# Cross attention on one core: another order of the first four blocks, with the division moved behind the values, seven-product projections from block 0, earlier loads and moves issued from two queues

## The chip, the core and the metric

The kernel runs on one core of a Trainium2 chip. The metric is device time in microseconds, the median of several runs. A core has five engines that work side by side and meet only through semaphores: TensorE (PE in the profile; its weight loads are listed apart as PEld), VectorE (DVE), ScalarE (ACT), GpSimd (POOL) and SyncE (SP, which here only issues transfers). Each engine executes its own queue strictly in the order in which the program was written, so an instruction that waits holds up all that stands behind it on the same engine. Transfers run on 16 DMA engines. PE writes to PSUM, eight banks of 128 partitions by 512 f32 numbers; the other data lie in SBUF.

## What is computed

Sixteen sequences x of 1024 rows by 512 features attend to 64 context rows each. Everything is f32. Cut to what matters:

```python
def _ada_ln(x, c, W_ss, b_ss):
    h = (x - mean(x)) / sqrt(var(x) + 1e-5)
    scale, bias = split(silu(c) @ W_ss + b_ss, 2)
    return (1.0 + scale)[:, None, :] * h + bias[:, None, :]

xq  = _ada_ln(x_q,  t_vec, Wss_q,  bss_q)
xkv = _ada_ln(x_kv, t_vec, Wss_kv, bss_kv)
q = (xq @ Wq + bq).reshape(B, Lq, 16, 32)
k, v = halves of (xkv @ Wkv + bkv), 16 heads of 32
scores = einsum('bqhd,bkhd->bhqk', q, k) / sqrt(32)
attn = softmax(scores)
out = einsum('bhqk,bkhd->bqhd', attn, v).reshape(B, Lq, 512)
return x_q + (out @ Wp + bp)
```

## The kernel before

**Tiling.** A block is 512 rows of x, so there are 32 blocks, two to a sequence. Keys and values are made for two sequences (four blocks) at a time. The work is software-pipelined: while block i is in its scores, block i-1 is multiplied with the values, block i-2 is projected, and blocks i+1 to i+5 are loaded, normalised, transposed and turned into queries. The schedule is written out by hand. It has three parts: the **way in** (lines 955 to 1136: the preparation and the scores of blocks 0 to 3), a loop `for i in range(4, NB - 2)` from line 1139 on, and a way out. The change edits the way in and a few helpers that it calls; loop and way out stay as they are.

**The steps of a block**, with the names that the schedule uses:

- `load_x(i)` loads 1 MB (tag `x`, two buffers); `load_residual(i)` loads the same rows again for the residual sum (tag `r`, two buffers). All loads are issued by SP.
- `q_stats(i)` computes mean and variance on DVE. `q_scale(i)` makes the reciprocal deviation: two or five small ACT steps, then four small steps on POOL (argument `apart` true) or on DVE. `hidden(i, ts)` normalises on ACT, in place, a quarter block at a time.
- `turn(i, ts)` transposes 32x32 squares on DVE into a tile `ht`; `move(i)` (line 502) then carries the squares to their partitions with 16 DMAs of 64 KB into `xt`, which holds features by rows.
- `queries(i, o)` (line 533) multiplies one quarter of the query features on PE and has ACT write it to `qt` (`queried`). The later form needs seven quarter-size products for the whole block instead of eight: `query_product(i, n)`, with sums of halves that `query_weight_sums` and `feature_sums` make on POOL, a seed copied by ACT (`query_seed`) and results read out by ACT (`query_out`) and DVE (`query_added`).
- `scores(i, z)` does half of the keys: PE writes two PSUM tiles of two banks (tag `s`, which has only two such tiles), DVE takes the maxima, ACT copies the scores to SBUF. `crossed=True` has ACT begin with the second tile while DVE begins with the first; on the same tile the two follow one another. `maxima(i)` joins the maxima and spreads them over a tile; `subtract(i)` subtracts them, on POOL or DVE, two operations of 128x2048; `weights(i, z)` is the exponential on ACT.
- The division of the softmax comes in two forms. **Before the values:** `sums` (DVE), `inverse` (DVE: reciprocal and a spread of 128x2048) and `divide` (POOL, two operations of 128x2048), then `mix(i)` multiplies with the values on PE and `mixed(i)` copies the result with ACT. **Behind the values:** `mix` takes undivided weights; meanwhile `total` (POOL) and `row_total` (DVE) sum them, `inverse_rows` takes reciprocals and brings them to their partitions through DRAM (one DMA out, four in), `spread_rows` spreads them on DVE and `divided(i)` multiplies on DVE while reading PSUM.
- The projection comes in two forms too. `project(i, t)` takes four steps of a quarter of the rows, each joined to the residual by DVE (`projected`), with the bias added to the residual rows by POOL (`residual`). The other form has **seven products**: `product(i, n)`, n = 1 to 7, in two accumulators, banks 2 and 3. `biased(i, k)` has ACT seed an accumulator with the bias (k = 2) or the difference of two bias halves (k = 3), `row_sums` makes sums of halves on POOL, and `added(i, n)` has DVE add the state of the accumulator to its part of the output after each product. So product n+1 in the same bank waits for `added(i, n)`. `weight_sums` prepares the weight sums once, on POOL.
- Banks 0 to 3 are dealt out by `ring`; once the seven-product projection runs, the ring is cut to banks 0 and 1.

**Where each form was used before the change.** Blocks 0 to 2 were divided before the values, blocks from 3 on behind them. Blocks 0 and 1 used `project`, blocks from 2 on the seven products. Blocks 0 to 4 used `queries`, blocks from 5 on the seven products. `load_x(3)`, `load_residual(0)` and the projection's weights and bias were loaded between `hidden(1)` and `queries(0, 2)`.

Of the kernel before, what the change touches and what calls it, by code (L numbers as in the profile page):

```python
# [9 lines left out]
F32 = mybir.dt.float32  # L10
# [5 lines left out]
P = 128  # L16
# [4 lines left out]
def cross_attention_block(  # L21
# [16 lines left out]
):  # L38

# [99 lines left out]
    def load_x(i):  # L139
        t = xpool.tile([P, NT, H], F32, tag="x", name=f"x_{i}")  # L140
        nc.sync.dma_start(t, rows_of(x, i))
        x_tiles[i] = t
# [34 lines left out]
    for c in range(NC):  # L177
        nc.sync.dma_start(
            b_v_sb[c * 32 : (c + 1) * 32, :],
            b_kv[H + c * P : H + (c + 1) * P].rearrange("(o h) -> o h", o=1).to_broadcast([32, P]),  # L180
        )
# [123 lines left out]
    def q_scale(i, kvb=None):  # L305
        n = NT if kvb is None else NT + 1
        q_rstd[i] = rstd_of(q_mv.pop(i)[:, :n, :], n, "q", i > 1)
        if kvb is not None:
            kv_rstd[kvb] = (q_rstd[i], NT)
# [180 lines left out]
    def turn(i, ts):  # L490

        if ts[0] == 0:
            ht_tiles[i] = hpool.tile([P, 4, NC, NT, 32], F32, tag="ht", name=f"ht_{i}")
# [8 lines left out]
    def move(i):  # L502
# [3 lines left out]
        for k in range(4):  # L506
            for g in range(4):
                nc.sync.dma_start(  # L508
# [24 lines left out]
    def queries(i, o, later=False):  # L533
        xt, b = xt_tiles[i], i // BPB
        w = wq_tiles.get(b, w_q_sb)
        if o == 0:

            tag = "vb" if i in (1, 3) else "qt"
            qt_tiles[i] = qpool.tile([P, NC, TB], F32, tag=tag, name=f"qt_{i}", bufs=1)
# [13 lines left out]
    def queried(i, o):  # L553
        pq, b = pq_tiles.pop((i, o)), i // BPB
        dst = qt_tiles[i][:, o, :]
# [194 lines left out]
    def inverse(i):  # L750
# [4 lines left out]
        vb_tiles[i] = spread(i, v, f"vb_{i}", other=i in (1, NB - 1))  # L755
# [15 lines left out]
    def row_total(i):  # L771
# [7 lines left out]
        )  # L779

# [187 lines left out]
    query_bias_rows()  # L968
    kv_stats(0)
# [10 lines left out]
    load_x(2)  # L980
    load_residual(0)
    load_projection_bias()
# [5 lines left out]
    load_x(3)  # L988
# [7 lines left out]
    keys(0)  # L996
    hidden(2, range(NT))


    scores(0, 0)  # L1000
    turn(2, range(NT))
    move(2)
    load_context(2)
    load_x(4)
    load_residual(1)
    residual(0)
    value_products(0)
    scores(0, 1)
    maxima(0)
    subtract(0, nc.vector, (0,))  # L1010
    value_tiles(0)
    subtract(0, nc.vector, (1,))
    queries(1, 0)
    query_weights(1)
    queries(1, 1)
    weights(0, 0)
    queries(1, 2)
    weights(0, 1)
    sums(0, 0)
    queries(1, 3)  # L1020
    query_weight_sums()
    sums(0, 1)
    inverse(0)
    divide(0)
    scores(1, 0)
    queries(2, 0)
    q_stats(3)
    queries(2, 1)
    q_scale(3)
    scores(1, 1)  # L1030
    maxima(1)
    subtract(1)
    queries(2, 2)
    hidden(3, (0, 1))
    mix(0, apart=False)
    mixed(0)
    hidden(3, (2, 3))
    queries(2, 3)
    turn(3, range(NT))
    move(3)  # L1040
    kv_stats(2)
    q_stats(4)
    project(0, 0)
    weights(1, 0)
    sums(1, 0)
    project(0, 1)
    weights(1, 1)
    residual(1)


    load_x(5)
    q_scale(4)
    kv_scale(2)
    scores(2, 0)
    sums(1, 1)
    inverse(1)
    divide(1)
    project(0, 2)
    context_hidden(2)
    hidden(4, (0, 1))  # L1060
    scores(2, 1)
    maxima(2)
    subtract(2)
    weight_sums()
    hidden(4, (2, 3))
    project(0, 3)
    queries(3, 0)
    queries(3, 1)
    queries(3, 2)
    turn(4, range(NT))  # L1070
    load_residual(2)
    move(4)
    mix(1)
    mixed(1)
    q_stats(5)
    weights(2, 0)
    queries(3, 3)
    project(1, 0)
    sums(2, 0)
    weights(2, 1)  # L1080
    project(1, 1)
    sums(2, 1)
    inverse(2)
    divide(2)
# [3 lines left out]
    project(1, 2)  # L1088


    load_x(6)
    scores(3, 0, crossed=True)
    project(1, 3)
    ring[:] = [0, 1]
    scores(3, 1)
    maxima(3)
    subtract(3)
    queries(4, 0)
    load_residual(3)
    hidden(5, (0, 1))  # L1100
    biased(2, 2)
    mix(2)
    mixed(2)
    hidden(5, (2, 3))
    q_stats(6)
    turn(5, range(NT))
    move(5)
    q_scale(6)
    row_sums(2, 0)
    load_x(7)  # L1110
    queries(4, 1)
# [3 lines left out]
    weights(3, 0)  # L1115
    added(2, 2)
    biased(2, 3)
    weights(3, 1)
    total(3)
    queries(4, 2)  # L1120
    keys(2)
    hidden(6, range(NT))
    scale_features(5)
    row_sums(2, 1)
# [209 lines left out]
```

## Time and profile before

| what | value |
|---|---|
| median of 3 runs | 1059.04 us (1056.97 to 1059.98) |
| the profiled execution | 1058.86 us |
| its span, first to last instruction | 1057.1 us |
| mean granted TensorE clock | 0.998 |
| DVE busy, 50 to 60 us and 100 to 110 us | 9.83 and 9.76 of 10 us |
| POOL busy, 10 to 30 us | 0 of 20 us |
| DMA share, 10 to 30 us | 1.04 |
| the loop's first scores, scores(4,0), start on PE | 161.96 us |

The page lists busy time per engine, the busy tenths of 40 slices of the span, the DMA queues, the chain of work that ended last (followed back from the last instruction, each step to what released it), and the costliest groups of instructions. A timeline shows instructions in the order of their start: start, length in us, engine, line, operation, output and inputs with their shapes, how many were merged (x), and in brackets how long the engine had been idle and what ended that. "PE busy" covers matmuls whose ends are modelled, so a busy PE can still wait a little inside a merged row. Times in tables and text count from the start of the span.

The chain of waits shows how closely the engines hang together at the beginning of the kernel (start us, us, what):

```
64.53 1.41 DVE vb L716
65.94 1.02 issue
66.96 0.02 POOLq L760
66.98 9.01 POOL s L760 x2
75.99 0.17 POOL workq L282
```

### The profile page before, as it was taken

The numbers are of one execution on the slowest core, as the hardware profiler recorded it, in microseconds if no ns is written. First come the engines' busy times: TensorE is split into PE (matmuls) and PEld (weight loads), VectorE is DVE, ScalarE is ACT, GpSimd is POOL, SyncE is SP. The second block draws the span as 40 slices with busy tenths as digits, with TensorE's granted clock in tenths as the row PEclk, the third lists the DMA queues.
The fourth block names the chain that finished last, engine by engine and source line by source line (L and its number), as shares of the span: only waits on it lengthen the run. The fifth ranks groups of instructions, "written<-read, shape, count | busy, mean of one in ns | idle before, by whom it ended". The sixth has DMA issues, their size and how long they took to land.

```text
span 1057.1 us, 22537 instructions
## 1 busy us (share of the span) xinstructions
PE 1033.6 (98%) x8914; PEld 733.7 (69%) x8914; DVE 854.7 (81%) x1134; ACT 618.0 (58%) x951; POOL 752.7 (71%) x470
## 2 busy tenths in 40 slices
PE   6999998999999999999999999999999999999998
PEld 4534365777777787777787787777777777777433
DVE  5698648987789877888878878898778887776993
ACT  3566665665575655667556666566566765565330
POOL 0258794889768869788668986688886886787340
PEclk9999999999999999999999999999999999999999
DMA  9743444444535344544345443444454443334202
GB/s 337 248 127 111 130 122 127 155 150 147 161 94 162 123 140 145 171 148 127 106 131 164 153 158 112 126 141 150 139 157 134 152 134 116 98 115 162 82 30 90
DMA packets 99976, 147.27 MB, mean 139 GB/s; under 512 B 29944, under 2 KB 30096, under 8 KB 99872
## 3 DMA queue, kind: packets, MB, share of 16 engines
q1 hardware_dynamic: 99872, 145.85, 43.5%
q8 instruction: 70, 1.15, 0.5%
q14 instruction: 34, 0.28, 0.1%
HBM read 78.85 MB, written 34.44 MB: 107 GB/s over the span
## 4 chain that ended last, share of the span: by engine, by line
PE 80%; DVE 5%; POOL 5%; DMA 4%; SPq 2%; issue 2%; ACT 1%; POOLq 0%; DVEq 0%; ACTq 0%
PE pp L933 28%; PE pq L625 27%; PE po L825 6%; PE ps L673 6%; PE pp L852 5%; PE pq L542 3%; SPq L508 2%; PE pv L431 2%; PE pk L395 2%; POOL s L760 2%; DMA wss_kv<-in_L_xcond_Wss_kv_dram 2%; DMA b_p_sb<-in_L_xcond_bp_dram 1%; POOL s L729 1%; DMA x<-in_x_dram 1%; DVE s L729 1%
## 5 line engine op out<-in xcount | busy, mean ns | idle before, releaser
L729 POOL TENSOR_TENSOR s<-s,mb 128x2048 f32<-128x2048 f32 x58 | 263.1, 4560 | 160.8 <-DVE mb L716 160.8
L694 ACT COPY s<-ps 128x1024 f32<-128x1024 f32 x128 | 129.5, 1012 | 119.7 <-DVE m L685 82.9
L685 DVE TRANSPOSE_TENSOR_REDUCE m<-ps 128x32 f32<-128x1024 f32 x128 | 150.6, 1214 | 27.1 <-PE ps L673 27.1
L655 ACT ACTIVATE qt<-pq,bias_t 128x256 f32<-128x256 f32 x208 | 85.8, 463 | 110.9 <-PE pq L625 110.9
L933 PE MATMUL pp<-w_p_sb,ot 128*128 128x256 f32 x648 | 148.7, 379 | 0.0
L735 ACT ACTIVATE s<-s 128x2048 f32<-128x2048 f32 x64 | 122.3, 1911 | 42.4 <-POOL s L729 31.8
L947 DVE TENSOR_TENSOR r<-pp,r 128x512 f32<-128x512 f32 x189 | 122.5, 670 | 25.5 <-PE pp L933 19.8
L933 PEld LDWEIGHTS pp<-w_p_sb,ot 128*128 128x128 f32 x648 | 123.4, 190 | 17.4 <-issue 0.7
L768 POOL TENSOR_TENSOR sum<-s,s 128x2048 f32<-128x2048 f32 x27 | 122.7, 4543 | 0.8 <-ACT s L735 0.8
L933 PEld LDWEIGHTS pp<-WT,s 128*128 128x128 f32 x432 | 78.9, 192 | 54.0 <-issue 29.3
L933 PE MATMUL pp<-WT,s 128*128 128x256 f32 x432 | 109.3, 397 | 0.0
L933 PE MATMUL pp<-WT,ot 128*128 128x256 f32 x432 | 102.2, 380 | 0.0
L625 PE MATMUL pq<-xt_sums,wq_sums 128*128 128x256 f32 x416 | 101.0, 386 | 0.0
L321 ACT ACTIVATE x<-x,rstdq 128x512 f32<-128x512 f32 x128 | 96.7, 807 | 4.8 <-POOL rstdq L285 3.2
L625 PE MATMUL pq<-xt,wq_sums 128*128 128x256 f32 x416 | 99.0, 381 | 0.0
L625 PEld LDWEIGHTS pq<-xt_sums,wq_sums 128*128 128x128 f32 x416 | 77.0, 190 | 31.1 <-issue 21.8
L625 PE MATMUL pq<-xt,w_q_sb 128*128 128x256 f32 x416 | 98.4, 380 | 0.1
L260 DVE BATCH_NORM_STATS2 bs<-x 128x6 f32<-128x512 f32 x128 | 86.9, 679 | 5.0 <-DMA x<-in_x_dram 5.0
L662 DVE TENSOR_TENSOR qt<-pq,qt 128x256 f32<-128x256 f32 x104 | 39.1, 418 | 63.1 <-PE pq L625 62.5
L933 PEld LDWEIGHTS pp<-WT,ot 128*128 128x128 f32 x432 | 82.2, 190 | 11.0
L565 ACT ACTIVATE xt<-xt,ss_q 128x512 f32<-128x512 f32 x112 | 84.7, 810 | 6.1 <-DMA xt<-ht 4.3
L625 PEld LDWEIGHTS pq<-xt,w_q_sb 128*128 128x128 f32 x416 | 79.1, 190 | 11.0 <-PE pp L933 0.4
(139 smaller groups left out, 1725.0 us busy)
## 6 DMA issues: line engine op xcount, KB each, us to landing
x<-in_x_dram SPq DMA_DIRECT2D x32, 1024.0 KB, 6.4
r<-in_x_dram SPq DMA_DIRECT2D x32, 1024.0 KB, 5.5
xt<-ht SPq DMA_DIRECT2D x496, 64.0 KB, 2.0
out_dram<-r SPq DMA_DIRECT2D x54, 512.0 KB, 3.8
out_dram<-r SPq DMA_DIRECT2D x20, 256.0 KB, 2.0
wss_q<-in_L_xcond_Wss_q_dram SPq DMA_DIRECT2D x2, 1024.0 KB, 8.8
ctx<-in_ctx_dram SPq DMA_DIRECT2D x8, 256.0 KB, 3.2
wss_kv<-in_L_xcond_Wss_kv_dram SPq DMA_DIRECT2D x2, 1024.0 KB
```

The source lines that it names most:

```text
L260: nc.vector.bn_stats(bs, r)
L321: nc.scalar.activation(dst, src, AF.Identity, bias=rstd[:, 1, j : j + 1], scale=rstd[:, 0, j : j + 1])
L565: nc.scalar.activation(xt[:, :, c, :], xt[:, :, c, :], AF.Identity, scale=ss["q"][:, c, b : b + 1], bias=ss["q"][:, NC + c, b : b + 1],)
L625: nc.tensor.matmul(qa[k][:, m * HT : (m + 1) * HT].rearrange("p (g n) -> p g n", g=2), lhsT=a[:, c, m * P : (m + 1) * P], rhs=x[:, :, c, : ...
L655: nc.scalar.activation(dst, src, AF.Identity, bias=bq_t[:, o : o + 1])
L685: nc.vector.tensor_reduce(m_tiles[i][:, z, 2 * e : 2 * e + 2, :], pss[e].rearrange("p r (j a) -> p r j a", a=32), AX.X, ALU.max, apply_tra ...
L694: nc.scalar.copy(s_sb[:, 2 * e : 2 * e + 2, :], pss[e])
L729: eng.tensor_tensor(s_tiles[i, z], s_tiles[i, z], mb_tiles[i], ALU.subtract)
L735: nc.scalar.activation(p, p, AF.Exp, scale=SCALE)
L768: nc.gpsimd.tensor_tensor(t, s_tiles[i, 0], s_tiles[i, 1], ALU.add)
L933: nc.tensor.matmul(acc[k][:, t * HO : (t + 1) * HO], lhsT=rows[:, c, t * P : (t + 1) * P], rhs=cols[:, c, :], start=n == 2 and t == 0 and ...
L947: nc.vector.tensor_add(r, acc[k].rearrange("p (t h) -> p t h", t=2), r)
```

## The change

Helpers:

```diff
     def load_x(i):
-        t = xpool.tile([P, NT, H], F32, tag="x", name=f"x_{i}")
+        t = xpool.tile([P, NT, H], F32, tag="r" if i == 3 else "x", name=f"x_{i}")
...
-    for c in range(NC):
-        nc.sync.dma_start(b_v_sb[...], b_kv[...].to_broadcast([32, P]))
+    def load_value_bias():
+        for c in range(NC):
+            b = b_kv[H + c * P : H + (c + 1) * P].rearrange("(o h) -> o h", o=1)
+            nc.sync.dma_start(b_v_sb[c * 32 : (c + 1) * 32, :], b.to_broadcast([32, P]))
...
-        q_rstd[i] = rstd_of(q_mv.pop(i)[:, :n, :], n, "q", i > 1)
+        q_rstd[i] = rstd_of(q_mv.pop(i)[:, :n, :], n, "q", i > 3)
...
     def turn(i, ts):
-            ht_tiles[i] = hpool.tile([P, 4, NC, NT, 32], F32, tag="ht", name=f"ht_{i}")
+            pool, tag = (big, "big2") if i == 2 else (hpool, "ht")
+            ht_tiles[i] = pool.tile([P, 4, NC, NT, 32], F32, tag=tag, name=f"ht_{i}")
...
     def move(i):
-                nc.sync.dma_start(
+                (nc.gpsimd if i < 4 and k % 2 else nc.sync).dma_start(
...
+    def halves_total(i):
+        lt_tiles[i] = small.tile([P, HPC, NJ], F32, tag="lt", name=f"lt_{i}")
+        both(lt_tiles[i].rearrange("p r j -> p (r j)"), l_tiles.pop(i), ALU.add)
```

The tile `qt` is now allocated in `queried(i, 0)` and not in `queries(i, 0)`; only block 1 takes the buffer `vb` for it, and only block 31 the buffer `xt` for its spread.

So 8 of the 16 transfers of move(1), move(2) and move(3) are issued by GpSimd; x_3 goes to a buffer of the residual rows and is loaded early; x_2 is queued ahead of the value bias; and the steps of `q_scale` for blocks 2 and 3 run on DVE instead of POOL. Blocks 0 and 1 still sum their weights half by half on DVE (`sums`), then `halves_total` joins the halves for the division behind the values; block 2 uses `total` and `row_total`.

The new order from the keys of block 0 to the loop (all of `inverse`, `divide`, `mixed`, `project`, `residual` and the four `queries(4, ...)` are gone from it):

```python
    key_products(0, bank("pk_0")); hidden(2, range(NT)); q_stats(3)
    turn(2, (0,)); key_tiles(0); turn(2, (1, 2, 3)); move(2)
    load_x(4); load_residual(0); load_context(2)
    q_scale(3); hidden(3, range(NT)); value_products(0); value_tiles(0)

    scores(0, 0, crossed=True); queries(1, 0); turn(3, (0, 1)); scores(0, 1)
    maxima(0); turn(3, (2, 3)); subtract(0, nc.vector)
    queries(1, 1); query_weights(1); weight_sums(); queries(1, 2); weights(0, 0)
    queries(1, 3); move(3); load_x(5); load_residual(1)
    weights(0, 1); query_weight_sums(); ring[:] = [0, 1]
    sums(0, 0); scores(1, 0, crossed=True); sums(0, 1); halves_total(0); inverse_rows(0)
    queries(2, 0); scores(1, 1); maxima(1); subtract(1); queries(2, 1); queries(2, 2)
    biased(0, 2); mix(0); spread_rows(0); divided(0)
    weights(1, 0); queries(2, 3); weights(1, 1); row_sums(0, 0)
    q_stats(4, kvb=2); q_scale(4, kvb=2)
    product(0, 1); added(0, 1); product(0, 2); added(0, 2); row_sums(0, 1); sums(1, 0)

    scores(2, 0, crossed=True); biased(0, 3); hidden(4, (0, 1))
    queries(3, 0, later=True); sums(1, 1); halves_total(1); inverse_rows(1)
    scores(2, 1); queried(3, 0); hidden(4, (2, 3)); maxima(2); subtract(2)
    product(0, 7); queries(3, 1); turn(4, range(NT)); move(4); load_x(6)
    added(0, 7); product(0, 6); added(0, 6); product(0, 5); added(0, 5)
    product(0, 4); added(0, 4); product(0, 3); added(0, 3); load_residual(2)
    biased(1, 2); mix(1); spread_rows(1); divided(1)
    context_hidden(2); queries(3, 2); weights(2, 0); row_sums(1, 0); q_stats(5)
    queries(3, 3); weights(2, 1); total(2); q_scale(5)
    context_features(2); scale_features(4)
    product(1, 1); added(1, 1); product(1, 2); added(1, 2); row_sums(1, 1)
    biased(1, 3); feature_sums(4); row_total(2); inverse_rows(2)

    scores(3, 0, crossed=True); product(1, 7); query_product(4, 1); query_seed(4)
    added(1, 7); scores(3, 1); hidden(5, (0, 1, 2)); product(1, 6); added(1, 6)
    maxima(3); subtract(3); query_product(4, 2); query_out(4, 2)
    product(1, 5); added(1, 5); product(1, 4); product(1, 3); hidden(5, (3,))
    spread_rows(2); added(1, 4); added(1, 3); biased(2, 2); load_residual(3)
    mix(2); divided(2); row_sums(2, 0); turn(5, range(NT)); move(5); load_x(7)
    query_product(4, 6); weights(3, 0); query_out(4, 6); q_stats(6)
    product(2, 1); added(2, 1); product(2, 2); added(2, 2); q_scale(6)
    weights(3, 1); total(3); query_product(4, 7); query_out(4, 7)
    biased(2, 3); row_sums(2, 1); key_products(2, spare("pk_2")); hidden(6, range(NT))
    query_product(4, 5); query_added(4, 5); key_tiles(2); turn(6, range(NT)); load_x(8)
    query_product(4, 4); query_added(4, 4); scale_features(5)
    value_products(2, spare("pv_2")); q_stats(7); value_tiles(2)
    query_product(4, 3); query_out(4, 3); feature_sums(5)
    product(2, 7); row_total(3); inverse_rows(3); move(6); q_scale(7)
```

(Several calls are put on one line here; the program has one to a line.)

Ahead of that, `load_x(2)`, `load_value_bias()` and `load_x(3)` stand right behind `query_bias_rows()`, and the projection's weights and bias are loaded behind `move(1)`.

## The prediction

> **What bounds the kernel now.** I read the page's busy shares and slices first, then each engine's timeline over 0 to 190 us; the loop over blocks 4 to 13 is not edited. TensorE (PE) is busy in 98% of the span, so little can be won unless its work or its few gaps shrink. The page, then PE's timeline (start, length, instructions, in brackets the idle time before them and what ended it):
>
> ```profile
> PE 1033.6 (98%) x8914; PEld 733.7 (69%) x8914; DVE 854.7 (81%) x1134; ACT 618.0 (58%) x951; POOL 752.7 (71%) x470
> ```
>
> ```profile
> 46.53 14.26 PE L542 MATMUL pq<-xt,wq 128*128 128x512 f32 x32 [0.97 <-DMA xt<-ht]
> ...
> 109.27 2.35 PE L825 MATMUL po<-s,vt 32*32 32x512 f32 x64
> ...
> 165.94 1.97 PE L625 MATMUL pq<-xt,w_q_sb 128*128 128x256 f32 x8
> 170.84 1.25 PE L673 MATMUL ps<-qt,kt 32*32 32x512 f32 x32 [2.94 <-ACT s L694]
> 172.02 3.56 PE L933 MATMUL pp<-WT,s 128*128 128x256 f32 x8
> ```
>
> The way in is already close to PE-bound: from 18.1 us to scores(4,0) at 161.96 PE shows about 6 us of gaps and stretched waits. Then 2.94 us pass before scores(4,1), and the next product takes 3.56 us where two take 3.45 elsewhere. The windows (length, busy time per engine, granted clock, DMA share, GB/s) say why: the clock was halved.
>
> ```profile
> 172.00:174.00 2.00, 2.00 (x12) 1.62 (x6) 2.00 (x3) 0.68 (x1) 0.00 (x0) 0.50 0.31 63
> ```
>
> What opens that gap is a chain from VectorE (DVE) over SyncE (SP): turn(5), 16 issues of move(5), then x_7, whose statistics stand in DVE's queue ahead of the maxima of scores(4,0):
>
> ```profile
> 143.31 2.49 DVE L495 STREAM_TRANSPOSE ht<-x 128x512 f32<-128x512 f32 x4 [0.19 <-ACT x L321]
> ...
> 161.90 0.69 DVE L260 BATCH_NORM_STATS2 bs<-x 128x6 f32<-128x512 f32 x1 [0.89 <-DMA x<-in_x_dram]
> ```
>
> ```profile
> 145.86 10.02 SPq L508 DMA_DIRECT2D xt<-ht  x16
> 155.97 5.43 SPq L141 DMA_DIRECT2D x<-in_x_dram  x2
> ```
>
> From the end of turn(5) (145.80) to scores(4,1) (170.84) it is 25.0 us; the new code has these steps in the same order.
>
> **Prices**, start to start in these timelines: a query chunk 3.55 (14.19/4); a product 1.77 (the loop takes 29.2 us a block; less scores 2.16 and mix 2.28, over 14 products); a project 3.5; a scores half 1.08; mix 2.28. On DVE: sums 2.2, a pair of maxima 2.3, spread 2.3, turn 2.45, added 0.65, q_stats 3.2. On ScalarE (ACT): exponential 1.85, a copy of scores 1.0. On POOL: a 128x2048 operation 4.5, a 128x512 one 1.27.
>
> **What goes.** Three stages become seven products: projections 0 and 1, query 4. Each saves 4x3.5-7x1.77 = 1.6 (query: 1.8), together 5.1 us of PE, 3.3 of it before mix(2). POOL loses two divisions (9.0 us) for each of blocks 0 to 2 and two residual additions (5.0 each). Most of that lay beside PE work: mix(0), mix(1) and mix(2) show about 1.5, 0 and 0.45 us of waiting, so it is worth 2 us, not 27.
>
> **What comes.** DVE gets divided (2.36 a block) where ACT copied, three more added per projection, and query_added. Two row sums and total(2) go to POOL, the accumulator seeds (0.57) to ACT. Loads of x_2 and x_3 are queued earlier, but the DMA engines moved 380 to 400 GB/s from 10 to 34 us: x_2 came 13 us after its issue, behind bytes that stay. I take 0.4 us earlier (0 to 1), and x_3 where r_0 came, by 38.
>
> **Moves from two queues.** 24 DMAs are issued by POOL; the trace has none there. Lower bound nothing; the nearest row is SP's 0.63 each; upper bound 2 us. [...] Then move(3) starts once queries(1,3) frees its buffer (62.2), its 8 issues and query_weight_sums (5.1) end at 75.3, and subtract(1), queued behind them, has its maxima at 75.9: free up to 1.07 us an issue. At 0.63 nothing changes. At 2 us subtract(1) is 7.4 late, less some 2 of slack: +5. [...] In the row above 8 issues fewer are 5 us. By the row move(1) lands 5 us earlier, [...] it removes at most the 0.97 at 46.53, because queries(1,0) now comes first at 44.
>
> **The walk**, each engine's new order laid out with those prices.
>
> Up to mix(0). x_2 lands 33.5; statistics 3.25, rstd 1.55, q_stats(3) 3.25, turn and key_tiles 3.2, rstd(3) 0.75: hidden(3) starts on ACT at 45.6 and holds it 2.9 us, with the copies of scores(0,0) queued behind. Those free the PSUM of scores(0,1) at 50.6, while PE finished queries(1,0) at 47.6: gap A, 2.9. Behind it the exponential delays queried(1,3): 1.2. Mix(0) ends at 78.6 (before: 78.37). The gaps of before (4.5 in all) were traded for as many.
>
> Mix(0) to mix(1). Work 3x3.55+7x1.77+2.16+2.28 = 27.5. DVE has spread_rows, divided, q_stats(4) with the context, two added and sums(1,0) before the maxima of scores(2,0): PE waits 1.2 before scores(2,1). Then gap D: product(0,5) reuses the bank that added(0,6) reads, and added(0,6) is queued behind sums(1,1), the inverse, maxima(2), the spread, turn(4) and added(0,7). From the end of the maxima of scores(2,0), DVE needs 2.2+0.9+2.3+0.3+2.35+2.4+1.2 = 11.7; PE has 1.08+1.77+3.55+1.77 = 8.2. D = 3.5, up to 3.9 with waits. I take 3.7: 32.4, against 33.2 before.
>
> Mix(1) to mix(2). Work 2x3.55+9x1.77+0.45+2.16+2.28 = 27.9. Gap E: product(1,7) needs biased(1,3), which stands in ACT's queue behind queried(3,3), weights(2,1), q_scale(5), context_features(2) and scale_features(4). These rows give most of it:
>
> ```profile
> 116.72 1.91 ACT L735 ACTIVATE s<-s 128x2048 f32<-128x2048 f32 x1 [0.75 <-POOL s L729]
> ...
> 122.59 2.47 ACT L380 ACTIVATE xk<-pkt,ss_kv 128x64 f32<-128x64 f32 x8 [2.92 <-PE pkt L348]
> 124.91 2.95 ACT L565 ACTIVATE xt<-xt,ss_q 128x512 f32<-128x512 f32 x4
> ```
>
> 0.65+1.85+1.15+2.4+2.9+0.57 = 9.5 after queries(3,3), against PE's 0.45+2x1.77+1.08 = 5.1: E = 4.4. In the old order only project(1,2) and project(1,3) stood there, which need no seed. Sum 32.3, against 27.2.
>
> Mix(2) to scores(4,1). Divided and turn(5) end 4.6 us after mix(2) (before 7.1: hidden(5) came late), then the chain of 25.0: 29.6, against 32.1. PE's own work there is 26.4, so it still waits about 3.
>
> Differences: +0.2-0.8+5.1-2.5 = +2.0.
>
> **The clock.** [...] By the row a gap of 2.94 sufficed; the gaps of at most 1.25 did not; half clock then lasted 3.4 us and cost 1.7. [...] by the row A is struck too. What A costs is mostly absorbed, since DVE leads there. Both D and E lie on PE's path: +3.4. The drop after the last gap is in both kernels.
>
> **Hand-overs.** The walk has no time between engines; the chain of waits of before shows 0.03 to 0.05 at each. Some 25 in the new path: +1.0.
>
> Sum +2.0+3.4+1.0 = +6.4. On the profiled execution (span 1057.1 and 1.8 around it, 1058.9) that is 1065.3; that run lies 0.2 under the median shown, 1059.04, less than the runs differ, so I leave it.
>
> **Rivals.**
> 1. D and E do not bite, because PE, not DVE and ACT, leads there: without them and their clock drops 11.5 us less, 1053.8. For it: PE led in 97 to 120 us before, where DVE once idled 8.4 us. Against: both gaps are differences of queues that start at the same event, so an early DVE doesn't remove them. 0.17.
> 2. The gaps come but the clock stays up (they are shorter, or split by instructions): 1065.3-3.4 = 1061.9; half of this case is within 0.3%. [...] against: the 2.94. 0.20.
> 3. POOL's descriptors cost 2 us each, and subtract(1) with all behind it comes 5 us late: 1070. For it: nothing in the trace bounds it above; against: 1.07 is free. 0.15.
> 4. The moves do not come sooner, DMA being the limit: by the above this changes less than 1 us and shares my forecast's number.
>
> **How the numbers follow.** My forecast, slower at 1065.3, has 0.48, its own range 1061 to 1069. What a measurement here can tell from no change is 0.3%, 3.2 us. Faster: rival 1, 0.17. Same: half of rival 2, the low edge of the forecast, 0.04, and the worst ends of rival 1 are left out: 0.14, with 0.03 for near misses 0.17. Slower: the rest, 0.66. The range takes rival 1's centre and rival 3's upper part: 1053.5 to 1073.
>
> **What would show it.** PE gaps over 3 us before product(0,5), ended by DVE's r, and before product(1,7), ended by ACT's pp; a granted clock of 0.5 after each; gap A ended by ACT's copies. Mix(2) should end near 148 (138.7 before) and turn(5) near 152. I am wrong if mix(2) ends before 142, if POOL's issues show over 1.3 us each with subtract(1) late, or if the gap before scores(4,1) has gone.

## The result: slower by 1.3%, and the profile after

| what | before | after |
|---|---|---|
| median of 4 runs each | 1058.01 us (1056.17 to 1059.98) | 1071.68 us (1069.82 to 1073.39) |
| ratio after to before, 95% interval | | 1.0129 (1.0101 to 1.0156) |
| the profiled execution, its span | 1058.86, 1057.1 us | 1071.24, 1069.5 us |
| mean granted TensorE clock | 0.998 | 0.989 |

The busy line of PE and the clock in 40 slices of the span, from the page of after:

```profile
PE 1035.9 (97%) x8986; PEld 750.3 (70%) x8986; DVE 864.5 (81%) x1156; ACT 612.9 (57%) x941; POOL 745.1 (70%) x481
...
PEclk9899988999999999999999999999999999999999
```

PE has less to multiply and is busy 2.3 us longer. The second line says why: three of the first seven slices (26.7 us each), the second, sixth and seventh, show an 8, and none after them does. PE's timeline of after, at its long gaps and at the rows that follow them (columns as before):

```profile
45.61 2.02 PE L677 MATMUL ps<-qt,kt 32*32 32x512 f32 x32 [2.96 <-DVE kt L409]
47.56 5.79 PE L542 MATMUL pq<-xt,wq 128*128 128x512 f32 x8
...
86.06 3.69 PE L941 MATMUL pp<-w_p_sb,ot 128*128 128x256 f32 x16 [1.55 <-DVE ot L813]
...
96.88 1.18 PE L677 MATMUL ps<-qt,kt 32*32 32x512 f32 x32 [2.42 <-ACT s L698]
...
108.58 2.58 PE L941 MATMUL pp<-WT,s 128*128 128x256 f32 x8 [3.44 <-DVE r L955]
110.95 3.03 PE L941 MATMUL pp<-w_p_sb,ot 128*128 128x256 f32 x8
...
134.40 3.75 PE L941 MATMUL pp<-WT,ot 128*128 128x256 f32 x8 [4.38 <-POOL s L920]
137.94 3.19 PE L629 MATMUL pq<-xt,w_q_sb 128*128 128x256 f32 x8
...
178.75 1.96 PE L677 MATMUL ps<-qt,kt 32*32 32x512 f32 x16 [2.78 <-DVE vt L447]
180.65 3.78 PE L941 MATMUL pp<-WT,s 128*128 128x256 f32 x8
...
186.40 1.14 PE L677 MATMUL ps<-qt,kt 32*32 32x512 f32 x32
```

The gaps D (3.44, before product(0,5)) and E (4.38, before product(1,7)) of the prediction are there. A gap of 2.96 before scores(0,0), one of 1.55 before product(0,1), and 1.2 of the 2.42 before scores(2,1) were not in it. The rows behind four of the gaps are stretched: a product takes 3.75 where 1.99 is normal. Four windows over those rows (window, length, busy time per engine, granted clock, DMA share, GB/s):

```profile
45.10:51.90 6.80, 6.29 (x37) 2.14 (x38) 4.72 (x12) 3.86 (x6) 3.98 (x9) 0.51 0.76 237
110.00:113.40 3.40, 3.40 (x10) 2.67 (x10) 0.69 (x1) 0.00 (x0) 3.40 (x1) 0.52 0.44 107
133.90:140.70 6.80, 6.30 (x15) 5.08 (x16) 4.09 (x5) 2.38 (x3) 6.49 (x6) 0.51 0.07 10
178.30:185.10 6.80, 6.35 (x27) 3.88 (x28) 5.94 (x7) 2.81 (x7) 1.95 (x5) 0.51 0.06 8
```

That is 23.8 us at half clock against 3.4 before. Half of such a stretch is lost if PE leads in it: at most 11.9 us against 1.7. Laid out by stage, with the ends of the mixes and the start of scores(4,1) from both timelines (all in us; the clock's share is half the length of the stretches in the stage, except in the first row, where the comparison under rows_later gives 0.2 instead of 3.4):

| stage | before | after | difference | clock's share | rest | predicted rest |
|---|---|---|---|---|---|---|
| to the end of mix(0) | 78.38 | 80.89 | +2.5 | +0.2 | +2.3 | +0.2 |
| to the end of mix(1) | 33.24 | 37.10 | +3.9 | +1.7 | +2.2 | -0.8 |
| to the end of mix(2) | 27.18 | 35.32 | +8.1 | +3.4 | +4.7 | +5.1 |
| to scores(4,1) | 32.04 | 33.09 | +1.1 | +3.4 | -2.3 | -2.5 |
| from there to the end | 886.26 | 883.10 | -3.2 | -1.7 | -1.5 | 0 |
| sum | 1057.1 | 1069.5 | +12.4 | +7.0 | +5.4 | +2.0 |

The prediction has 1.0 more for hand-overs, and 3.4 for the clock. Its third and fourth rows are right within 0.4; the first is 2.1 too low, the second 3.0 and the clock 3.6.

The unpredicted gap before product(0,1) begins in SP's queue. Its timeline in after: the loads of x_5 and r_1 (2 MB together), then the way out (`ltd`) and in (`vr`) of the reciprocals of block 0:

```profile
70.04 0.53 SPq L143 DMA_DIRECT2D x<-in_x_dram  x1
70.66 0.50 SPq L150 DMA_DIRECT2D r<-in_x_dram  x1
72.77 0.34 SPq L795 DMA_DIRECT2D ltd<-lt  x1
78.54 2.40 SPq L797 DMA_DIRECT2D vr<-ltd  x4
```

The way in needs what the way out has written. It was issued 5.77 us after it, and `spread_rows(0)` began on DVE at 82.28, 9.5 us after the way out, having waited 4.64 for it; the prediction has no term for this. As to the start, x_3 had not landed by 38: DVE shows its statistics standing at the head of the queue, and with them the keys for scores(0,0):

```profile
41.10 0.69 DVE L263 BATCH_NORM_STATS2 bs<-x 128x6 f32<-128x512 f32 x1 [2.01 <-DMA x<-in_x_dram]
...
44.91 0.65 DVE L409 TENSOR_TENSOR kt<-pk,bias_t 128x512 f32<-128x512 f32 x1
```

### The profile page after: what moved, and what is told of

It is laid out like the page before. It is cut to its first block, busy times and chain, and to the rows that moved or that the text cites. A ratio compares the mean times of both kernels' runs of the same rounds, so it can differ in the third digit from the quotient of the medians.

```text
span 1069.5 us, 22761 instructions
## 1 busy us (share of the span) xinstructions
PE 1035.9 (97%) x8986; PEld 750.3 (70%) x8986; DVE 864.5 (81%) x1156; ACT 612.9 (57%) x941; POOL 745.1 (70%) x481
## 4 chain that ended last, share of the span: by engine, by line
PE 84%; DVE 7%; DMA 4%; POOL 2%; SPq 2%; issue 1%; ACT 1%; DVEq 0%; POOLq 0%
PE pp L941 32%; PE pq L629 29%; PE po L833 6%; PE ps L677 6%; PE pp L860 3%; DMA x<-in_x_dram 3%; PE pq L542 2%; PE pv L434 2%; PE pk L398 2%; DVE m L689 1%; DVE bs L263 1%; SPq L512 1%; DVE s L733 1%; POOL sum L772 1%; DVE l L744 1%
## 5 line engine op out<-in xcount | busy, mean ns | idle before, releaser
L689 DVE TRANSPOSE_TENSOR_REDUCE m<-ps 128x32 f32<-128x1024 f32 x128 | 150.6, 1214 | 32.3 <-PE ps L677 30.4
L941 PE MATMUL pp<-w_p_sb,ot 128*128 128x256 f32 x696 | 160.9, 381 | 1.5 <-DVE ot L813 1.5
L955 DVE TENSOR_TENSOR r<-pp,r 128x512 f32<-128x512 f32 x203 | 132.0, 671 | 35.5 <-PE pp L941 27.7
L659 ACT ACTIVATE qt<-pq,bias_t 128x256 f32<-128x256 f32 x216 | 88.9, 462 | 110.4 <-PE pq L629 110.4
L941 PEld LDWEIGHTS pp<-w_p_sb,ot 128*128 128x128 f32 x696 | 133.1, 191 | 21.1 <-ACT qt L564 2.3
L941 PEld LDWEIGHTS pp<-WT,s 128*128 128x128 f32 x464 | 84.8, 192 | 60.8 <-issue 32.3
L941 PE MATMUL pp<-WT,s 128*128 128x256 f32 x464 | 117.8, 398 | 3.4 <-DVE r L955 3.4
L941 PE MATMUL pp<-WT,ot 128*128 128x256 f32 x464 | 111.6, 384 | 4.4 <-POOL s L920 4.4
L629 PE MATMUL pq<-xt,w_q_sb 128*128 128x256 f32 x432 | 103.7, 384 | 0.0
L629 PEld LDWEIGHTS pq<-xt_sums,wq_sums 128*128 128x128 f32 x432 | 79.8, 190 | 32.4 <-issue 21.8
L941 PEld LDWEIGHTS pp<-WT,ot 128*128 128x128 f32 x464 | 89.1, 192 | 18.4 <-issue 6.1
L629 PEld LDWEIGHTS pq<-xt,w_q_sb 128*128 128x128 f32 x432 | 83.6, 193 | 11.9
L629 PEld LDWEIGHTS pq<-xt,wq_sums 128*128 128x128 f32 x432 | 80.5, 190 | 11.5 <-issue 1.4
```

Of the source, the lines that this page charges most:

```text
L629: nc.tensor.matmul(qa[k][:, m * HT : (m + 1) * HT].rearrange("p (g n) -> p g n", g=2), lhsT=a[:, c, m * P : (m + 1) * P], rhs=x[:, :, c, : ...
L659: nc.scalar.activation(dst, src, AF.Identity, bias=bq_t[:, o : o + 1])
L689: nc.vector.tensor_reduce(m_tiles[i][:, z, 2 * e : 2 * e + 2, :], pss[e].rearrange("p r (j a) -> p r j a", a=32), AX.X, ALU.max, apply_tra ...
L941: nc.tensor.matmul(acc[k][:, t * HO : (t + 1) * HO], lhsT=rows[:, c, t * P : (t + 1) * P], rhs=cols[:, c, :], start=n == 2 and t == 0 and ...
L955: nc.vector.tensor_add(r, acc[k].rearrange("p (t h) -> p t h", t=2), r)
```

## The experiments

Each kernel is the changed one with the edit shown; all ratios are against the kernel before, on the same chip (its medians there: 1058.28 to 1058.68), with the 95% interval. "Half clock" sums the stretches of 0.5 in the clock records of the one execution that was profiled, without the last, at the very end of each trace. It differs between executions of one kernel: 35 of the kernel before, beside exp_later, had mean clocks of 0.995 to 1.000 and took 1055.88 to 1061.20 us. In loads_behind the profiled execution, 1069.00 us, was the slowest of its four.

| kernel | median us | runs | ratio to before | half clock us |
|---|---|---|---|---|
| turn_behind | 1066.45 | 6 | 1.0064 (1.0041 to 1.0088) | 17.1 |
| seed_ahead | 1066.52 | 4 | 1.0071 (1.0051 to 1.0090) | 10.2 |
| rows_later | 1067.52 | 4 | 1.0079 (1.0052 to 1.0105) | 13.7 |
| filler | 1066.33 | 5 | 1.0074 (1.0048 to 1.0100) | 10.2 |
| one_queue | 1075.69 | 4 | 1.0170 (1.0153 to 1.0187) | 23.9 |
| loads_behind | 1064.96 | 4 | 1.0055 (1.0038 to 1.0071) | 20.5 |
| stats_behind | 1063.99 | 4 | 1.0050 (1.0036 to 1.0064) | 10.2 |
| together | 1056.97 | 14 | 0.9988 (0.9977 to 0.9998) | 6.8 |
| exp_later | 1059.57 | 20 | 1.0017 (1.0007 to 1.0028) | 10.2 |
| exp_sooner | 1053.44 | 6 | 0.9959 (0.9944 to 0.9973) | 3.4 |
| all_seven | 1056.78 | 13 | 0.9989 (0.9981 to 0.9997) | 6.8 |
| sums_last | 1053.07 | 5 | 0.9953 (0.9939 to 0.9966) | 0 |

Of the times expected below only that of exp_sooner was met. The other single edits came out 0.5 to 3.0 us faster than expected, except one_queue, which was 2.2 slower; together, exp_later, all_seven and sums_last were 1.1 to 4.8 slower than hoped for.

**turn_behind: what is gap D?** The turn of block 4 goes behind the addition that product(0,5) waits for.

```diff
-    product(0, 7); queries(3, 1); turn(4, range(NT)); move(4); load_x(6)
-    added(0, 7); product(0, 6); added(0, 6); product(0, 5); added(0, 5)
+    product(0, 7); queries(3, 1); added(0, 7); product(0, 6); added(0, 6)
+    turn(4, range(NT)); move(4); load_x(6); product(0, 5); added(0, 5)
```

> Only turn(4), move(4) and load_x(6) go behind added(0,6); nothing else is moved. If product(0,5) was held because added(0,6) stood behind turn(4) in VectorE's queue (my theory), the gap of 3.44 us before product(0,5) shrinks to about 1.1 (added(0,7) and added(0,6) still follow the spread) and the granted clock stays at 1.0 there, so mix(1) starts about 4.0 us earlier (3.44-1.1 and 1.7 of half clock); the kernel about 3 to 4 us faster than the changed one, 1067.5 to 1068.5. Rival, the row sums of GpSimd or the projection itself hold it: the gap stays above 3 us and the time does not move.

PE's timeline of turn_behind, before product(0,1) and at product(0,5):

```profile
85.20 5.38 PE L941 MATMUL pp<-w_p_sb,ot 128*128 128x256 f32 x16 [2.01 <-DVE ot L813]
...
105.35 1.99 PE L941 MATMUL pp<-WT,s 128*128 128x256 f32 x8 [1.07 <-DVE r L955]
```

D shrinks from 3.44 to 1.07, by about the length of the turn (2.45), and product(0,5) runs at full speed: D is DVE's order, as worked out. mix(1) comes at 110.73, not 115.64. The row above it was not foreseen: here a gap of 2.01 before the first two products was followed by half clock (5.38 for what takes 3.69 in after), so the edit removed one loss of clock and this run has another.

**seed_ahead: who ends gap E?** Here prediction and profile disagree: the prediction named ACT's seed, the row of after POOL's L920. Both were done almost at once, on ACT and on POOL:

```profile
133.65 0.60 ACT L904 COPY pp<-b_diff 128x512 f32<-128x512 f32 x1
```

```profile
133.12 1.27 POOL L920 TENSOR_TENSOR s<-ot,s 128x512 f32<-128x512 f32 x1
```

The seed ends at 134.25, POOL's sum at 134.39, and product(1,7) begins at 134.40. The edit brings the seed forward alone:

```diff
-    context_features(2); scale_features(4)
-    product(1, 1); added(1, 1); product(1, 2); added(1, 2); row_sums(1, 1)
-    biased(1, 3); feature_sums(4); row_total(2); inverse_rows(2)
+    context_features(2)
+    product(1, 1); added(1, 1); product(1, 2); added(1, 2)
+    biased(1, 3); scale_features(4); row_sums(1, 1)
+    feature_sums(4); row_total(2); inverse_rows(2)
```

> Only biased(1,3) is moved, ahead of scale_features(4) in ScalarE's queue. My theory, that the seed held product(1,7): it starts about 131.5 instead of 134.4, then query_product(4,1) waits for scale_features to 134.4; both gaps are under 2 us, the clock stays at 1.0, scores(3,1) starts 3.5 to 5 us earlier; time 1067 to 1068. Rival, what the trace names, that GpSimd's row_sums(1,1) behind total(2) held it (it ended at the same moment): product(1,7) still starts at 134.4, the clock still drops, time within 1 us of the changed kernel's 1071.7.

PE and then POOL in seed_ahead:

```profile
129.96 1.97 PE L941 MATMUL pp<-WT,ot 128*128 128x256 f32 x8 [1.58 <-ACT pp L904]
...
135.67 1.17 PE L677 MATMUL ps<-qt,kt 32*32 32x512 f32 x32 [2.02 <-ACT s L698]
```

```profile
131.48 1.28 POOL L920 TENSOR_TENSOR s<-ot,s 128x512 f32<-128x512 f32 x1
```

Product(1,7) now starts 1.5 us before L920 does, so it never needed it: the seed held it, and POOL was named because it ended last. E falls from 4.38 to 1.58 and the clock stays full; 2.02 of waiting comes in before scores(3,1): ACT's copy, which frees the PSUM tile, began behind DVE's maxima, and these stood behind `row_total(2)`, which had waited 2.53 us for POOL's sum.

**filler: gap or clock?** Four matmuls of 128x512 that nobody reads are put into gap E; the gap itself stays.

```diff
     scores(3, 0, crossed=True)
+    dummy = bank("dummy", 1)
+    for c in range(NC):
+        nc.tensor.matmul(dummy, lhsT=w_q_sb[:, c, :P], rhs=w_kv_sb[:, c, :TB],
+                         start=(c == 0), stop=(c == NC - 1))
     product(1, 7)
```

> Adds four matmuls of 128x512 (3.5 us) that nobody reads, in the gap between scores(3,0) and product(1,7); the wait itself is untouched, so TensorE has more to do. By the clock theory (a gap of about 3 us and more halves the clock afterwards for 3.4 to 6.8 us) product(1,7) starts at 134.4 as before but runs at full clock: product(1,7) and query_product(4,1) take 1.8 each, not 3.5 and 3.1, and the kernel is 3 us FASTER, about 1068.5. If the long products are something else [...], the time stays at 1071.7 or rises.

PE in filler, from the added matmuls on, and the granted clock of a window behind them (columns as above):

```profile
128.46 3.70 PE L1124 MATMUL dummy<-w_kv_sb,w_q_sb 128*128 128x512 f32 x8
132.92 1.96 PE L941 MATMUL pp<-WT,ot 128*128 128x256 f32 x8 [0.75 <-ACT pp L904]
134.72 1.89 PE L629 MATMUL pq<-xt,w_q_sb 128*128 128x256 f32 x8
```

```profile
132.00:137.00 5.00, 4.25 (x35) 3.19 (x48) 4.41 (x5) 3.15 (x5) 4.76 (x5) 1.00 0.12 32
```

The figures in the expectation are those of the traces: half clock of 3.4 us stood behind the gap of 2.94 in before and behind D (3.44) in after, 6.8 us of it behind E (4.38). Here PE does more work and the kernel is 5.3 us faster than after (1066.33 against 1071.68; its five executions range from 1063.22 to 1070.61). Product(1,7) starts about 4.4 us after scores(3,0) in both; only the two rows behind it are shorter, 3.85 against 6.94 us together. From mix(1) to mix(2) filler takes 32.3 us and after 35.3. The remaining 2.3 lie elsewhere: filler's profiled run also has no half clock behind D (1.7), though nothing was changed there.

**rows_later: the late x_3.** The keys come ahead of the statistics of block 3, whose normalisation moves behind scores(0,1).

```diff
-    key_products(0, bank("pk_0")); hidden(2, range(NT)); q_stats(3)
-    turn(2, (0,)); key_tiles(0); turn(2, (1, 2, 3)); move(2)
+    key_products(0, bank("pk_0")); hidden(2, range(NT))
+    key_tiles(0); turn(2, range(NT)); move(2)
...
-    q_scale(3); hidden(3, range(NT)); value_products(0); value_tiles(0)
-    scores(0, 0, crossed=True); queries(1, 0); turn(3, (0, 1)); scores(0, 1)
-    maxima(0); turn(3, (2, 3)); subtract(0, nc.vector)
+    value_products(0); value_tiles(0)
+    scores(0, 0, crossed=True); queries(1, 0); q_stats(3); scores(0, 1)
+    q_scale(3); hidden(3, range(NT)); maxima(0); subtract(0, nc.vector)
+    turn(3, range(NT))
```

> key_tiles(0) and turn(2) go ahead of the statistics of block 3, and these, q_scale(3), hidden(3) and turn(3) go behind the scores of block 0. If the late landing of x_3 (41.05) held VectorE's queue and so scores(0,0): the gap of 2.96 before scores(0,0) and its 6.8 us of half clock go, scores(0,1) starts near 48 instead of 53.3 and scores(1,0) near 61 instead of 64.9; behind that VectorE leads, so the kernel gains about 3 us: 1068 to 1069. Rival, move(1) is what comes late: scores(0,0) starts earlier but queries(1,0) waits for xt and nothing is gained.

scores(0,0) starts at 43.60 and scores(0,1) at 48.32, both without a wait (before the edit 45.61 and 53.29). But PE's timeline of rows_later then has

```profile
64.03 1.72 PE L677 MATMUL ps<-qt,kt 32*32 32x512 f32 x26 [1.33 <-ACT qt L564]
```

with a wait of 0.73 just ahead of it and half clock from 64.46 to 67.87, and mix(0) starts at 78.52; in after it is 78.54. What PE gains at 44 to 53 us it loses before scores(1,0): on ACT the normalisation of block 3 now stands ahead of the query copies and the exponentials.

This does not show that gap A and the late rows cost nothing, for the edit sets new losses in their place. In turn_behind, seed_ahead, filler and stats_behind, PE's program up to mix(0) is that of after. PE at scores(0,1) in seed_ahead, then in stats_behind:

```profile
50.76 1.47 PE L677 MATMUL ps<-qt,kt 32*32 32x512 f32 x32 [2.42 <-ACT s L698]
```

```profile
49.20 1.47 PE L677 MATMUL ps<-qt,kt 32*32 32x512 f32 x32 [0.84 <-ACT s L698]
```

In both, scores(0,0) starts at 43.6 and no half clock falls before mix(0), which starts at 76.33 and 74.78: the 1.6 us less of gap A arrive whole. In after, x_3 and with it scores(0,0) came 2.1 us later than in seed_ahead, and mix(0) 2.2 later. After's half clock at 45 us cost next to nothing, since it took the place of gap A: from scores(0,0) to mix(0) it is 32.93 against 32.78 in seed_ahead. But a stretch of 3.4 us of it behind gap A, at 51 to 56 us, cost its full 1.7 in turn_behind and filler (34.48 and 34.43). Of the 4.2 us by which rows_later is faster than after, its trace puts none before mix(0).

**one_queue: do the moves matter?** All 16 DMAs of each move are issued by SP again.

```diff
-                (nc.gpsimd if i < 4 and k % 2 else nc.sync).dma_start(
+                nc.sync.dma_start(
```

> Only the issue of move(1), move(2), move(3) goes back to SyncE alone. Theory: the second queue saves issue time but nothing waits for it, and GpSimd's packets of move(1) even pass ahead of x_3. Then x_3 lands at 38 to 39 instead of 41, the gap before scores(0,0) shrinks from 2.96 to under 1.5, queries(1,0) waits up to 2 us for move(1) instead, and the time is within 2 us of the changed kernel, 1069.5 to 1073.5. Rival, the second queue is what the early stage needs: move(1) lands 4 to 5 us later and the time rises by 2 us or more. If the second queue is itself what made the change slower, the time falls by over 4 us.

It is 4.0 us slower than after. SP's queue and PE's row of product(0,1) in one_queue:

```profile
63.12 10.74 SPq L512 DMA_DIRECT2D xt<-ht  x16
...
75.25 0.46 SPq L795 DMA_DIRECT2D ltd<-lt  x1
83.44 1.76 SPq L797 DMA_DIRECT2D vr<-ltd  x4
```

```profile
90.32 6.40 PE L941 MATMUL pp<-w_p_sb,ot 128*128 128x256 f32 x16 [7.64 <-DVE ot L813]
```

The query stages show no loss: mix(0) starts even earlier (76.70). What suffers is the small transfer behind the moves: 16 issues of 0.67 us hold SP to 73.9, the loads follow, and the way in of the reciprocals is issued 4.9 us later than in after. The gap grows from 1.55 to 7.64, and 10.2 us of half clock begin in it.

**loads_behind: the round trip.** The two loads are issued behind it.

```diff
-    queries(1, 3); move(3); load_x(5); load_residual(1)
+    queries(1, 3); move(3)
...
     sums(0, 0); scores(1, 0, crossed=True); sums(0, 1); halves_total(0); inverse_rows(0)
+    load_x(5); load_residual(1)
```

> load_x(5) and load_residual(1) go behind inverse_rows(0) on SyncE. Theory: the 2 MB ahead of it in the DMA rings made the round trip of the reciprocals take 10 us instead of 5 to 6. Then vr lands by 78 instead of 82, the gap of 1.55 before product(0,1) goes and that before scores(2,1) shrinks from 2.4 to about 1, mix(1) starts 2.5 to 3 us earlier, time 1068 to 1069.5. Rival, the round trip is slow for other reasons or VectorE comes late anyway: time unchanged within 1 us.

SP's queue in loads_behind:

```profile
72.49 0.35 SPq L795 DMA_DIRECT2D ltd<-lt  x1
73.96 1.76 SPq L797 DMA_DIRECT2D vr<-ltd  x4
```

The way in follows the way out after 1.47 us instead of 5.77; `spread_rows(0)` starts at 77.28, the gap before product(0,1) is gone, and the one before scores(2,1) is 0.47, not 2.42. mix(1) comes 2.7 us earlier.

**stats_behind: the wait inside scores(4,0).** The 2.78 there are for the spare PSUM tile of `value_products`, which `value_tiles(2)` has to read out; it stands behind the statistics of block 7 on DVE, and these wait for x_7. DVE in after:

```profile
174.67 0.69 DVE L263 BATCH_NORM_STATS2 bs<-x 128x6 f32<-128x512 f32 x1 [0.89 <-DMA x<-in_x_dram]
...
177.89 0.72 DVE L447 TENSOR_TENSOR vt<-pv,b_v_sb 128x256 f32<-128x256 f32 x2
```

```diff
-    q_stats(7); value_tiles(2)
+    value_tiles(2)
...
-    move(6); q_scale(7)
+    move(6)
...
         scores(i, 1)
+        if i == 4:
+            q_stats(7); q_scale(7)
         product(b, 5)
```

> The statistics of block 7 (and q_scale(7)) go behind scores(4,1), into the loop's first round, and value_tiles(2) no longer stands behind them. Theory: the chain turn(5), move(5), x_7, statistics is what holds the entry into the loop. Then the gap of 2.78 inside scores(4,0) and its half clock go, scores(4,1) starts 5 to 7 us earlier, time 1065 to 1067. Rival, the chain is covered by later waits (the loop then waits for hidden(7) or for the maxima): under 2 us gained.

PE in stats_behind:

```profile
170.41 1.62 PE L677 MATMUL ps<-qt,kt 32*32 32x512 f32 x32 [1.33 <-ACT qt L659]
```

1.33 is left of the wait, no half clock follows, and from mix(2) to mix(3) it is 39.6 us against 43.6.

**together: all five,** turn_behind, seed_ahead, rows_later, loads_behind and stats_behind.

> turn_behind, seed_ahead, rows_later, loads_behind and stats_behind at once. If the slowdown is the sum of queue waits and of the half clock after them, and the 5.1 us of TensorE work are really saved, then all clock drops of the way in are gone and the kernel is faster than both: 1049 to 1055. If removing one wait only uncovers the next (VectorE as the bound of the way in), it stays at 1056 to 1062.

1056.97: 14.7 us less than after, and level with before (ratio 0.9988). The five single gains add up to 29.0, about twice as much. That they are not additive fits what the single profiles show: each also won or lost half clock at places that its edit didn't touch. Left were waits of 0.73 and 1.33 in scores(1,0), 1.07 before product(0,5), 1.58 before product(1,7) and 2.02 before scores(3,1), with 3.4 us of half clock behind the scores of block 1 and behind the last of these.

**exp_later, exp_sooner, all_seven: the waits that are left.** exp_later starts from together and keeps block 3 out of ACT's and DVE's way before scores(1,0):

```diff
-    q_stats(3); scores(0, 1); q_scale(3); hidden(3, range(NT)); maxima(0)
-    subtract(0, nc.vector); turn(3, range(NT)); queries(1, 1); query_weights(1)
-    weight_sums(); queries(1, 2); weights(0, 0); queries(1, 3); move(3); weights(0, 1)
-    query_weight_sums(); ring[:] = [0, 1]; sums(0, 0); scores(1, 0, crossed=True)
-    sums(0, 1); halves_total(0); inverse_rows(0); load_x(5)
+    q_stats(3); scores(0, 1); maxima(0); q_scale(3); subtract(0, nc.vector)
+    queries(1, 1); queries(1, 2); weight_sums(); query_weights(1); queries(1, 3)
+    weights(0, 0); weights(0, 1); ring[:] = [0, 1]; sums(0, 0); scores(1, 0, crossed=True)
+    hidden(3, range(NT)); sums(0, 1); halves_total(0); inverse_rows(0)
+    turn(3, range(NT)); move(3); query_weight_sums(); load_x(5)
```

> together, and hidden(3), turn(3), move(3) go behind the first scores of block 1, queries(1,3) ahead of weights(0,0). Theory: what is left before scores(1,0) in together (about 3.1 us of waiting and 1.7 of half clock) is ScalarE's queue, hidden(3) and query_weights(1) ahead of the exponentials and of queried(1,3). Then scores(1,0) starts within 0.7 us after queries(1,3), mix(0) 3 to 4 us earlier than 78.8, time 1052 to 1055. Rival, VectorE leads there: mix(0) moves by under 1 us, time stays at 1056 to 1058.

exp_sooner starts from together as well and takes the exponential of block 2 out of the queue ahead of the seed:

```diff
     product(0, 5); added(0, 5)
+    weights(2, 0)
...
-    biased(1, 2); mix(1); spread_rows(1); divided(1)
-    context_hidden(2); queries(3, 2); weights(2, 0); row_sums(1, 0); q_stats(5)
-    queries(3, 3); weights(2, 1); total(2); q_scale(5)
+    biased(1, 2); weights(2, 1); mix(1); total(2); spread_rows(1); divided(1)
+    context_hidden(2); queries(3, 2); row_sums(1, 0); q_stats(5)
+    queries(3, 3); q_scale(5)
```

> together, and the exponentials of block 2 go into ScalarE's idle stretch before mix(1), total(2) right behind mix(1). Theory: ScalarE's queue from queries(3,3) to the copies of scores(3,0) sets the gaps of 1.6 before product(1,7) and 2.0 before scores(3,1) and their half clock. Then both fall below 1 us, mix(2) comes 3 to 4 us earlier against mix(1), time 1053 to 1055. Rival, VectorE's maxima behind row_total(2) hold scores(3,1): row_total(2) is earlier too, so only a gap of about 1 us stays; if both gaps stay, the time does not move.

all_seven has both edits:

> exp_later and exp_sooner together. If the 5.1 us less of TensorE work are there to be had and only waits hid them, this is the first version clearly faster than the kernel before: 1048 to 1052, ratio 0.990 to 0.994. If each removed wait uncovers another, it stays at 1054 to 1057.

exp_sooner works, 3.5 us better than together. Its PE timeline:

```profile
120.53 1.97 PE L941 MATMUL pp<-WT,ot 128*128 128x256 f32 x8 [0.43 <-ACT pp L904]
...
125.10 1.47 PE L677 MATMUL ps<-qt,kt 32*32 32x512 f32 x32 [0.88 <-ACT s L698]
```

Both gaps are under 1 us and the half clock behind them has gone. exp_later is 2.6 us worse than together. mix(0) does start 4.0 earlier (74.79), and it is all lost again; POOL's, ACT's and PE's timelines of exp_later:

```profile
80.78 1.27 POOL L592 TENSOR_TENSOR wq_sums<-w_q_sb,wq_sums 128x512 f32<-128x512 f32 x1
82.01 9.02 POOL L733 TENSOR_TENSOR s<-s,mb 128x2048 f32<-128x2048 f32 x2
```

```profile
86.57 1.91 ACT L739 ACTIVATE s<-s 128x2048 f32<-128x2048 f32 x1 [9.13 <-POOL s L733]
88.39 0.67 ACT L564 ACTIVATE qt<-pq,bqs 128x512 f32<-128x512 f32 x1
```

```profile
89.11 2.00 PE L677 MATMUL ps<-qt,kt 32*32 32x512 f32 x26 [2.99 <-ACT qt L564]
```

I had put the issues of move(3) and the weight sums ahead of `subtract(1)` on POOL. The exponential waited 9.13 us for it, the query copy stood behind the exponential on ACT, and scores(2,0) waited for the copy; 6.8 us of half clock came on top. all_seven inherits this (the stretch at 88.9) and so is no better than together.

**sums_last: the same without that wait.** all_seven with the weight sums behind the last row sums of block 0, ahead of their first user.

```diff
-    turn(3, range(NT)); move(3); query_weight_sums(); load_x(5)
+    turn(3, range(NT)); move(3); load_x(5)
...
-    row_sums(0, 1)
+    row_sums(0, 1); query_weight_sums()
```

> all_seven with query_weight_sums behind row_sums(0,1) on GpSimd. Theory: in exp_later and all_seven mix(0) did come 4 us earlier, but move(3) and the four weight sums then stood ahead of subtract(1) on GpSimd (it began at 82.0 instead of 77.1), and queried(2,3) behind weights(1,0) on ScalarE held scores(2,0) for 2.99 us. Then subtract(1) begins 4 to 5 us earlier, that gap and its 6.8 us of half clock go, time 1049 to 1052, ratio near 0.992. Rival, VectorE's spread or the turn of block 3 holds subtract(1): it begins at 80 or later and the time stays at 1055 to 1057.

POOL in sums_last, and PE's busy line and clock from its page:

```profile
76.85 9.04 POOL L733 TENSOR_TENSOR s<-s,mb 128x2048 f32<-128x2048 f32 x2 [0.60 <-ACT pp L904]
```

```profile
PE 1026.3 (98%) x8986; PEld 744.8 (71%) x8986; DVE 864.5 (82%) x1156; ACT 612.4 (58%) x941; POOL 745.2 (71%) x481
...
PEclk9999999999999999999999999999999999999999
```

The subtraction starts 5.2 us sooner than in exp_later, the wait before scores(2,0) has gone, and no half clock is left. It takes 1053.07 us, 5.3 less than before and 18.6 less than after; the 1049 to 1052 expected were not reached. Between it and exp_sooner (1053.44) no difference can be told: its mix(0) starts 2.3 us earlier, but 2.08 us of waiting before scores(2,1) follow and its mix(1) starts 0.2 later (105.94 against 105.73). So the edit of exp_later gains nothing, even without that wait. PE is busy 1026.3 us; before, less the 1.7 of its half clock, it was 1031.9. The 5.6 between them agree with the 5.1 of work that the change was worked out to save.

## Why the prediction was right, and by how much it was off

Slower was forecast, and the median is 1.3% slower, 6.4 us above the forecast of 1065.3. That is above the forecast's own range (1061 to 1069) and inside the whole one (1053.5 to 1073), whose upper end was set for rival 3, which fell. The way it went and the two gaps were worked out; that three terms sized too low stayed within the range is in part luck.

- **What goes:** 5.1 us of PE work; sums_last agrees (5.6). In after it cannot show, because PE waits and runs at half clock.
- **Gap D:** 3.7 predicted, 3.44 measured; turn_behind shows its cause. **Gap E:** 4.4 and 4.38; seed_ahead shows that it was ACT's seed, as worked out, against the name in the profile.
- **Up to mix(0):** its end was put at 78.6 and came at 80.89. x_3 was taken to land by 38 and its statistics began at 41.1. In turn_behind and seed_ahead, with the same order there, scores(0,0) waited only 0.65, gap A then was 2.42 (predicted 2.9), ended by ACT's copies as forecast, and mix(0) ended at 79.57 and 78.68. In after the late rows replace gap A. That DVE leads there, so that what the clock loses at A is mostly absorbed, was right for after's stretch alone (0.15 lost); behind gap A the stretch cost all of its 1.7.
- **Mix(0) to mix(1):** 32.4 without the clock was predicted, 37.1 less 1.7 measured: 3.0 too little. The missing term is the round trip of the reciprocals, at which the prediction puts nothing: it took 9.5 us behind 2 MB of loads. In loads_behind it took at most 4.8, and the stage is 2.5 shorter though it has 3.4 us more of half clock; less its clock it is 31.2.
- **POOL's issues:** from nothing to 2 us each was allowed for, the upper end an assumption of mine that no row had shown; at SP's 0.63, the nearest row, nothing was to change. POOL's timeline of after has eight of them in one row, 0.51 us each:

```profile
31.30 4.11 POOL L512 DMA_DIRECT2D xt<-ht  x8 [29.99 <-DVE ht L499]
```

  Rival 3 falls.
- **The moves from two queues,** rival 4: "changes less than 1 us" was wrong; without it the kernel is 4.0 us slower (1075.69 against 1071.68). In one_queue, where they are issued by SP alone, mix(0) came no later for it. What I left out was what stands behind the 16 issues in SP's queue, the reciprocals of block 0, whose way in was issued at 83.44 instead of 78.54. Issue time was what counted: the moves of block 3 held SP for 10.74 us there and for 4.97 in after.
- **Mix(2) to scores(4,1):** 29.6 predicted; 33.1 less the 3.4 of clock is 29.7. Mix(2) itself ended at 153.3, where 148 was forecast.
- **The clock,** the most mis-sized term: +3.4 predicted, +7.0 measured. I gave each of D and E one stretch of 3.4 us, the length of the one that stands in before, none to the start, and took the last as equal in both kernels. Measured were 3.4 behind D and 6.8 behind E, at the start and at the last gap; they are counted at half their length, but for the start's. In filler gap E stayed, filled, and its half clock went (product(1,7) took 1.96, not 3.75). Rival 2, a clock that stays up, falls, and rival 1 with it.

So the 6.4 are the clock (3.6), the round trip (3.0), x_3 (2.1) and 0.4 between the median and the profiled run, less 2.7 by which the rest came out lower. Of these, 1.0 are the hand-overs and 1.5 fell behind scores(4,1), most of them inside the loop; why is open. After's x_3 was the latest of the traces that share its order, so its 2.1 are in part this one execution's.

## What to carry to other kernels

Where a tight engine loses clock after a wait, price a gap at its own length plus the stretch of slow clock that may follow it (3.4 to 10.2 us here, half of it lost where PE leads), and close gaps of 2 us too (2.01 was followed by one in turn_behind). When an operation is moved, look up what stands behind it in every queue, of small transfers above all: a 32 KB round trip behind two large loads, a seed behind a normalisation and a subtraction behind weight sums cost 6.7, 5.2 and 3.7 us of the median here (loads_behind and seed_ahead against after, sums_last against all_seven), while the work saved was 5.1 in all. Reordering by such rows turned a loss of 13.7 us into a gain of 5.3 with the same arithmetic.

## What the runs showed of the hardware that I had not expected

- **The length of a gap alone does not decide whether the clock falls.** Behind the gap of 3.44 before product(0,5) there was half clock in after, seed_ahead and loads_behind (the product took 2.58, 3.16 and 3.78); in filler and stats_behind it took 1.99, full speed, behind the same 3.44. Behind gaps of 2.01, 2.04 and 2.08 before product(0,1) there was half clock in turn_behind, stats_behind and filler (5.38 for the first two products), and none behind 2.11 in seed_ahead, where the same two took 3.69. Behind gap E (4.38 or 4.39) there was half clock in all six kernels that kept it unfilled: product(1,7) took 3.26 to 3.75, against 1.96 in filler.

  The slow stretches in the way in of the profiled runs last 3.4, 6.8 or 10.2 us; in after they begin at 44.99, 109.84, 133.74 and 178.11. What decides besides the length was not shown: no run shifted a gap and nothing else.
- **GpSimd is held only about 0.5 us by the issue of a DMA of 64 KB** (0.49 to 0.51 in after); SP's eight issues in the same three moves took 1.32, 0.63 and 0.62 each.
- **A small round trip through DRAM** had its second half issued 1.5 us after the first with a free queue (loads_behind), and 5.8 and 8.2 us after it (after, one_queue) behind two loads of 1 MB.
